# Graph attention, first layer: large piece buffers 7 to 6, small piece buffers 3 to 4, transposed adjacency tiles 3 to 4

## The chip, the cores and the metric

The kernel runs on one core of one Trainium2 chip. Its engines are TensorE (PE in the profile), VectorE (DVE), ScalarE (ACT), GpSimd (POOL) and SyncE (SP, which issues transfers). The metric is the device time of one execution in microseconds; lower is better. Three runs of the kernel before took 3587.35, 3585.51 and 3601.4 us; their median is 3587.35.

## The reference

A graph network of four layers on 3327 nodes with 512 features and a dense 0/1 adjacency matrix. Every layer is `x = x + gnn(relu(layernorm(x)))`. Layers 0 to 2 are graph attention with 8, 4 and 8 heads; layer 3 is a mean over neighbours. The first layer, which the change touches, is

```python
Wh = jnp.einsum('nd,hdo->hno', x, W)             # 8 heads of 64
f1 = jnp.einsum('hno,ho->hn', Wh, a1)
f2 = jnp.einsum('hno,ho->hn', Wh, a2)
e = jax.nn.leaky_relu(f1[:, :, None] + f2[:, None, :], negative_slope=0.2)
e = jnp.where(adj[None, :, :] > 0, e, NEG_INF)
h_prime = jnp.einsum('hnm,hmo->hno', jax.nn.softmax(e, axis=-1), Wh)
out = jax.nn.elu(h_prime)
```

Layer 1 is the same with self loops added to the adjacency and 128 features in each of 4 heads; layer 2 is as layer 0 on other weights; layer 3 multiplies the 0/1 mask with x, divides by the degree and applies three dense matrices.

## The kernel before

**Tiles.** The 3327 nodes make 26 tiles of 128 (the last holds 127). Rows (the attending nodes) are worked off in seven chunks `c`: six of four tiles and one of two. Columns (the attended nodes, tiles `j`) come in five groups `g` of 6, 6, 6, 4 and 4 tiles, the list `JG`; a group of six is called large here, one of four small.

**How softmax becomes matmuls.** The exponential of a leaky relu of a sum is one of two products, depending on the sign of the sum. So `matrices` makes, for a head, a chunk and a group, two 0/2 masks in fp8: `tht` (an edge, and the sum is positive) and `gt` (an edge, and it is not). First `compare` compares the score row `s1b` (a score for each row of the chunk, broadcast over partitions, loaded by `score_rows`, L676) with the column's own score: on ScalarE (L664), for some tiles on VectorE (L661). Then two bitwise operations on VectorE against the adjacency mask `m` split the result: L668 writes `tht`, L670 rewrites `gt`. TensorE multiplies `tht` (L760) and `gt` (L763) with the *pieces*: the features of the column nodes times the two exponentials, each written as three bf16 numbers that add up to the f32 value, so 195 columns for each mask. The pieces of a layer lie in DRAM, a block for each head and group.

**Loops.** For each chunk and each head the five piece blocks are loaded (L714), large groups into tiles with the tag `ab` (600 KB each), small ones into tiles with the tag `abx` (400 KB each). `pieces_tile` chooses the tag: `abx` for a group of four tiles in layer 0, but not for the first head, whose pieces are put together on the chip (`ahead`) and lie in `ab` tiles for all five groups. Then come two passes over the 26 column tiles, one for the first two row tiles of the chunk and one for the other two. Only the very first head of the first chunk is cut in four passes (the last group starts later there). A pass of a full chunk has 104 matmuls, a head 208. A buffer of pieces comes free when the second pass has done its last matmul with it. VectorE then reduces the sums (L778), scales them and divides (L796 to L803) into the chunk's rows `A`.

**What runs beside it.** After each pass `hooks.run` gives out other work: the node stages of the next layer for rows that are done (norm, projection, pieces of the next layer), and in layer 0 the making of the adjacency masks for the next chunk (`mask_steps`): a load of a piece of the adjacency matrix as bf16 (`at`, three buffers, issued by GpSimd, L226), for chunks after the first a transposing DMA into `tr` (issued by SP, L238; the first chunk is transposed by TensorE), a comparison on VectorE (`st`, L245; for a tile on the diagonal also L250 and L251), and a store to DRAM (L252). The masks of a chunk are read back into `m` tiles by SP (L265).

**What sets the order.** The engines run in order. The order on each engine is made when the program is built: a planner takes instructions by their place in the code as soon as their inputs and buffers are free in its own estimate of time. `after(inst, name)` holds an instruction back until another one has been placed; most of the side work is tied in this way to the last matmul of the pass that has just ended (`gone[-1]`). SP's queue carries the loads of pieces, score rows and masks, the transposes, the stores of masks and of the next layer's pieces; an instruction at its head that waits holds up all that follows.

**Memory.** A partition's memory is given out as a stack of pools. `pieces` (the `ab` tiles of layer 0) and `masks` (`at`, `st`, `d`) stand below the pool `first` (the node work before the attention) and, after that is closed, below `att0` (the tiles of layer 0's attention, laid out in the order `A`, `R`, `tht`, `tr`, `abx`, `gt`). After layer 0 all of them are closed, and layer 1's tiles (`att1`) lie on the same addresses; a tile there waits for the tiles below it that were in use.

Of the kernel before, what the change touches and what calls it, by code (L numbers as in the profile page):

```python
# [26 lines left out]
BF16 = mybir.dt.bfloat16  # L27
# [10 lines left out]
P = 128  # L38
# [14 lines left out]
def tile_gnn(ctx: ExitStack, tc: tile.TileContext, x, adj, W0, a01, W1, al, ar, W2, a2,  # L53
# [7 lines left out]
    def pn(t):  # L61
        return min(P, N - t * P)
# [5 lines left out]
    JM = max(n for _, n in JG)  # L68
# [36 lines left out]
    def dims(l):  # L105


        H = heads[l]
        DA = D // H + 1
        AO = -(-(3 * DA + 1) // 8) * 8 if l != 1 else 3 * DA + 1  # L110
        return H, DA, AO, 2 * AO

    abd = []
    for l in range(3):
        H, DA, AO, HW = dims(l)
# [29 lines left out]
    def after(inst, name):  # L145

        tc.add_manual_dep(inst.ins, name, mybir.DependencyInfo(mybir.DependencyClass.NoSync,
                                                               mybir.DependencyReason.SCHED_ONLY))
# [62 lines left out]
    def mask_steps(pool, t, g):  # L211


        n = pn(t)
        c, k = where[t]
        j0, nj = JG[g]
        w = min(nj * P, N - j0 * P)
        q = {}

        def load():  # L220
            at = q["at"] = pool.tile([P, JM * P], BF16, name="at", bufs=3)
            if n < P:
                nc.vector.memset(at, 0.0)
            elif w < nj * P:
                nc.vector.memset(at[:, w:nj * P], 0.0)
            ld = nc.gpsimd.dma_start(at[:n, :w], adj[t * P:t * P + n, j0 * P:j0 * P + w])  # L226
            after(ld, gone[-1] if gone else stored[NT - 1] if c else relus[-3])

        def turn():
            at = q["at"]  # L230
            if c == 0:
                tp = q["tp"] = ps.tile([P, 8, P], BF16, name="tp", bufs=2)
                for j in range(nj):
                    nc.tensor.transpose(tp[:, j, :], at[:, j * P:(j + 1) * P], identb)
                compare()
            else:
                tp = q["tp"] = mp.tile([P, JM, P], BF16, name="tr", bufs=3)
                tr = nc.sync.dma_start(tp[:, :nj], at[:, :nj * P], transpose=True)  # L238
                after(tr, gone[-1] if gone else stored[NT - 1])

        def compare():
            hooks.done += 1
            tp = q["tp"]
            st = masks0[g][:, k] if c == 0 else pool.tile([P, JM, P], FP8, name="st", bufs=3)[:, :nj]
            cm = nc.vector.tensor_scalar(st, tp[:, :nj], 0.0, 2.0, op0=ALU.is_gt, op1=ALU.mult, saturate=False)  # L245
            if gone:
                after(cm, gone[-1])
            if j0 <= t < j0 + nj:
                d = pool.tile([P, P], BF16, name="d", bufs=1)
                nc.vector.tensor_tensor(d, tp[:, t - j0, :], negI, ALU.is_gt)  # L250
                nc.vector.tensor_scalar(dg1[:, t, :], d, 2.0, None, op0=ALU.mult, saturate=False)  # L251
            nc.sync.dma_start(maskd[c][g][:, k], st)  # L252
        return (load, turn) if c == 0 else (load, turn, compare)

    def mask_view(c, g):
# [107 lines left out]
    def pieces(L, t, AB, pool, first, behind=None):  # L363
# [29 lines left out]
        if o == two - 1 and l == 1:  # L393
            for a in range(2):
                L.to_store.append((abd[l][g][:, a, :, js, :].rearrange("h p j w -> p h j w"), pt[:, :, a]))
        elif first and o == two - 1:
            if g not in ahead:
                ahead[g] = pieces_tile(L, bp, g)
            nc.sync.dma_start(ahead[g][:, js], pt[:, 0])
            stored[t] = nc.sync.dma_start(abd[l][g][:, :, js, :].rearrange("h p j w -> p h j w"), pt).ins.name  # L400
        elif o == two - 1:
            L.to_store.append((abd[l][g][:, :, js, :].rearrange("h p j w -> p h j w"), pt))
# [236 lines left out]
    def pieces_tile(L, pool, g):  # L639

        nj = JG[g][1]
        HW = dims(L.l)[3]
        if L.l == 0 and nj == 4 and gone:
            tl = mp.tile([P, nj * HW], BF16, name="abx", bufs=3)
        else:
            tl = pool.tile([P, JM * HW], BF16, name="ab", bufs=7)
        return tl[:, :nj * HW].rearrange("p (j w) -> p j w", j=nj)

    def matrices(L, nt, h, g, s1v, mask, pt, gt):
# [29 lines left out]
    def attention(L, hooks, open_next, close):  # L679
# [5 lines left out]
        for c, (t0, nt) in enumerate(chunks):  # L685
# [3 lines left out]
            for h in range(H):  # L689
# [10 lines left out]
                for a in range(2 if l == 1 else 1):  # L700
                    row = []
                    for g, (_, nj) in enumerate(JG):
                        if l == 1:
                            tl = mp.tile([P, JM * 2 * DA], F32R, name="ab", bufs=7)
                            two = KIND[g] != "b"
                            w = 2 * DA if two else AO
                            v = (tl if two else tl.bitcast(BF16))[:, :nj * w].rearrange("p (j w) -> p j w", j=nj)
                            ld = nc.sync.dma_start(v.bitcast(F32) if two else v, abd[l][g][h, a])
                        else:
                            if g in ahead:  # L710
                                v = ahead.pop(g)
                            else:
                                v = pieces_tile(L, mp if l else bp, g)
                                ld = nc.sync.dma_start(v, abd[l][g][h])  # L714
                        row.append(v)
                    ab.append(row)
# [152 lines left out]
    def lay_out(pool, *tags):  # L869
        for name, n, dt, bufs in tags:  # L870
            pool.tile([P, n], dt, name=name, bufs=bufs)
# [15 lines left out]
    lay_out(rp, ("s1b", WMAX, F32, 2))  # L887
    masking = ExitStack()
    bp = masking.enter_context(tc.tile_pool(name="pieces", bufs=1))
    lay_out(bp, ("ab", JM * 400, BF16, 7))  # L890
    ip = masking.enter_context(tc.tile_pool(name="masks", bufs=1))
    with tc.tile_pool(name="first", bufs=1) as fp:

# [18 lines left out]
        L = open_layer(0)  # L912
# [27 lines left out]
        while hooks.small:  # L940
            hooks.small.pop(0)()
    A, R = [("A", D, F32, n) for n in A_BUFS], ("R", PER * 2 * 129, F32, 1)
    ab, gt, tht = ("ab", JM * 400, BF16, 7), ("gt", PER * JM * P, FP8, 7), ("tht", PER * JM * P, FP8, 7)
    tags = [[A[0], R, tht, ("tr", JM * P, BF16, 3), ("abx", 4 * 400, BF16, 3), gt],
            [A[1], ("ab", JM * 258, F32R, 7), R, ("ts", 2 * JM * P, F32R, 3), ("tv", 2 * 4 * P, F32R, 2), tht[:3] + (10,)],
            [A[2], ab, ("R", PER * 2 * 65, F32, 1), tht, gt]]
    hooks.masks = in_steps([mask_steps(ip, t, g) for t, g in order[20:]])
    for l in range(3):
# [3 lines left out]
        mp = att.enter_context(tc.tile_pool(name=f"att{l}", bufs=1, reuse_waits="tile"))  # L952
# [13 lines left out]
        L = nxt[0]  # L966
# [512 lines left out]
```

## Time and profile before

| what | value |
|---|---|
| median of three runs | 3587.35 us (3585.51 to 3601.4) |
| the profiled execution's own time | 3590.36 us |
| its span | 3588.6 us, mean granted TensorE clock 0.988 |
| TensorE busy | 3452.1 us (96%) |
| weight loads busy | 3112.2 us (87%) |
| VectorE, ScalarE, GpSimd busy | 2622.2, 2507.9, 632.5 us |
| moved by DMA | 797.72 MB, 222 GB/s over the span |
| loads of large pieces in layer 0 and 2 (600 KB, `ab`, SP) | 333, median 5.2 us to landing |
| loads of small pieces in layer 0 (400 KB, `abx`, SP) | 110, median 6.9 us to landing |
| transposing DMAs (`tr`, SP) | 110, median 5.9 us to landing |

How to read it: the profile has a page with the busy time of each engine, the span in 40 slices, the DMA queues, the chain of work that ended last, and the costliest groups of instructions. A group is named by its line, engine, operation and tiles (out<-in). Other views list the instructions of one tile, who waited for whom, the instructions in order of time (start, duration, and in brackets the idle time before one and what ended it), and the busy time of all engines in chosen stretches. Layer 0's attention runs from 163 us to 1249 us of the span, layer 1 from there to about 2090, layer 2 to about 3240, and the last layer's sums to the end. The granted clock is the share of TensorE's full speed that was allowed in a stretch.

### The profile page before, as it was taken

To read this page: it belongs to the slowest core of one execution; us is meant where nothing else is said; L and a number is where in the kernel's file an instruction comes from. 1 tells how busy PE (TensorE), PEld (TensorE's weight loads), DVE (VectorE), ACT (ScalarE), POOL (GpSimd) and SP (SyncE) were. 2 spreads that over 40 slices of the span, in tenths; PEclk is the share of its full clock that TensorE was granted. 3 is DMA by queue.
4 is the path that set the end of the run, shared out by engine and by line. 5 is a ranking of instruction groups with operands and counts; after the bars stand their busy time and mean duration, and the time that the engine had idled before them with its cause. 6 is when DMAs were issued, how large, how long until landed. Compare 5 with 4: busy or idle time off the path is not lost. (4 is left out here: it accounts for less than half of the span.)

```text
span 3588.6 us, 77637 instructions
## 1 busy us (share of the span) xinstructions
PE 3452.1 (96%) x30751; PEld 3112.2 (87%) x30751; DVE 2622.2 (73%) x5227; ACT 2507.9 (70%) x4113; POOL 632.5 (18%) x858
## 2 busy tenths in 40 slices
PE   7889999999999999999999989999999999999998
PEld 6788999999999878888888869989898989876887
DVE  8777878787887789888888868877676767672221
ACT  5767877877887888888798767766676667572111
POOL 6601222111110211233223230001010101020000
PEclk9999999999999999999999999999999999999999
DMA  7798999999966877777877876655555555576331
GB/s 216 235 239 222 237 249 233 258 236 242 262 217 207 283 277 262 282 258 273 283 256 266 307 280 212 195 174 178 176 195 176 173 178 184 166 264 257 122 99 60
DMA packets 398119, 797.72 MB, mean 222 GB/s; under 512 B 112969, under 2 KB 221844, under 8 KB 397104
## 3 DMA queue, kind: packets, MB, share of 16 engines
q1 hardware_dynamic: 363890, 723.14, 62.5%
q0 software_dynamic: 28128, 62.42, 7.5%
q10 hardware_dynamic: 5726, 7.08, 0.6%
q8 instruction: 245, 4.01, 0.5%
q14 instruction: 130, 1.06, 0.1%
HBM read 663.59 MB, written 129.64 MB: 221 GB/s over the span
## 5 line engine op out<-in xcount | busy, mean ns | idle before, releaser
L664 ACT ACTIVATE gt<-s1b,ks 128x512 fp8e4<-128x512 f32 (+1 forms) x2448 | 1448.0, 677 | 294.3 <-issue 160.1
L760 PE MATMUL acc<-ab,tht 128*128 128x195 bf16 (+1 forms) x9112 | 1558.0, 248 | 11.3 <-DVE tht L668 9.2
L763 PE MATMUL acc<-ab,gt 128*128 128x195 bf16 (+1 forms) x9112 | 1557.1, 248 | 5.7 <-DVE rc L800 3.3
L763 PEld LDWEIGHTS <-gt 128*128 128x128 fp8e4 x10744 | 1055.5, 98 | 64.3 <-issue 41.5
L760 PEld LDWEIGHTS <-tht 128*128 128x128 fp8e4 x10744 | 1055.2, 98 | 35.2 <-DVE tht L668 20.0
L668 DVE TENSOR_TENSOR tht<-gt,m 128x768 uint32<-128x768 uint32 (+3 forms) x557 | 449.8, 808 | 121.8 <-ACT gt L664 120.1
L670 DVE TENSOR_TENSOR gt<-tht,m 128x768 uint32<-128x768 uint32 (+3 forms) x557 | 450.1, 808 | 8.7
L633 ACT CAST ts<-tht 128x1536 fp32r<-128x1536 fp8e4 x208 | 300.0, 1470 | 59.0 <-PE acc L753 54.9
L753 PE MATMUL acc<-ab,ts 128*128 128x258 f32 x2496 | 335.0, 290 | 4.9 <-DMA ab<-ab 2.5
L753 PEld LDWEIGHTS acc<-ab,ts 128*128 128x128 f32 x2496 | 314.6, 191 | 14.4 <-issue 3.3
L661 DVE TENSOR_SCALAR gt<-s1b,ns 128x512 fp8e4<-128x512 f32 (+1 forms) x446 | 217.3, 492 | 133.6 <-PE acc L763 127.9
L1015 PE MATMUL acc<-y,mf 128*128 128x512 f32 x1352 | 309.9, 391 | 2.3 <-DVE mf L1010 2.3
L664 ACT ACTIVATE tht<-s1b,ks 128x512 fp8e4<-128x512 f32 (+1 forms) x504 | 308.3, 680 | 2.9 <-DMA s1b<-s 2.4
L763 PE MATMUL acc<-abx,gt 128*128 128x195 bf16 (+1 forms) x1632 | 288.7, 250 | 20.8 <-DVE rc L800 7.8
L760 PE MATMUL acc<-abx,tht 128*128 128x195 bf16 (+1 forms) x1632 | 289.5, 250 | 19.3 <-DMA abx<-ab 15.5
L1015 PEld LDWEIGHTS acc<-y,mf 128*128 128x128 f32 x1352 | 253.6, 188 | 58.5 <-DVE mf L1010 2.7
L863 POOL TENSOR_TENSOR xt<-xt,e 128x512 f32<-128x512 f32 x72 | 122.1, 1695 | 899.6 <-DVE e L862 586.4
L778 DVE TENSOR_REDUCE R<-acc 128x130 f32<-128x390 f32 x416 | 214.7, 556 | 77.5 <-PE acc L763 76.9
L756 PE MATMUL acc<-ab,tht 128*128 128x387 bf16 x1248 | 226.6, 330 | 9.0 <-DMA ab<-ab 5.4
L1012 ACT CAST mf<-m 128x768 fp32r<-128x768 fp8e4 (+1 forms) x78 | 59.1, 762 | 245.8 <-PE acc L1015 234.0
L753 PE MATMUL acc<-ab,tv 128*128 128x258 f32 x1664 | 219.3, 283 | 2.5 <-DVE tv L633 1.4
L753 PEld LDWEIGHTS acc<-ab,tv 128*128 128x128 f32 x1664 | 207.3, 189 | 4.7 <-DVE tv L633 2.5
(163 smaller groups left out, 3722.6 us busy)
## 6 DMA issues: line engine op xcount, KB each, us to landing
ab<-ab SPq DMA_DIRECT2D x333, 600.0 KB, 5.2
ab<-ab SPq DMA_DIRECT2D x112, 774.0 KB, 6.6
ab<-ab SPq DMA_DIRECT2D x112, 516.0 KB, 5.4
ab<-ab SPq DMA_DIRECT2D x112, 400.0 KB, 3.8
abx<-ab SPq DMA_DIRECT2D x110, 400.0 KB, 6.9
ab<-ab SPq DMA_DIRECT2D x56, 582.0 KB, 7.3
s1b<-s SPq DMA_DIRECT2D x120, 256.0 KB, 6.4
m<-mask SPq DMA_DIRECT2D x69, 384.0 KB, 4.1
```

Of the source, the lines that this page charges most:

```text
L633: (nc.scalar.copy if KIND[g] == "s" else nc.vector.tensor_copy)(t[:, :k1 - k0, :nj], th[a][g][:, k0:k1])
L661: nc.vector.tensor_scalar(gv[:, :, jj, :], s1v, L.ns2[:, j, h:h + 1], 2.0, op0=ALU.is_gt, op1=ALU.mult, saturate=False)
L664: nc.scalar.activation(gv[:, :, jj, :], s1v, AF.Relu, bias=L.ks2[:, j, h:h + 1], scale=BIG, saturate=False)
L668: nc.vector.tensor_tensor(pu, gu, mu, ALU.bitwise_and)
L670: nc.vector.tensor_tensor(gu, pu, mu, ALU.bitwise_xor)
L753: mm = nc.tensor.matmul(acc[k][:, :2 * DA], thr[g][:, k - ks[0], jj, :], ab[a][g][:, jj, :], start=(j == 0), stop=(j == NT - 1), skip_grou ...
L756: mm = nc.tensor.matmul(acc[k][:, :3 * DA], th[a][g][:, k, jj, :], ab[a][g][:, jj, :3 * DA], start=(j == 0), stop=(j == NT - 1), skip_grou ...
L760: nc.tensor.matmul(acc[k][:, :3 * DA + o], th[0][g][:, k, jj, :], ab[0][g][:, jj, :3 * DA + o], start=(j == 0), stop=False, skip_group_che ...
L763: mm = nc.tensor.matmul(acc[k][:, AO:AO + 3 * DA + o], th[1][g][:, k, jj, :], ab[0][g][:, jj, AO:AO + 3 * DA + o], start=False, stop=(j == ...
L778: nc.vector.tensor_reduce(R[:, k], v.rearrange("p a (s d) -> p a d s", s=3), AX.X, ALU.add)
L863: nc.gpsimd.tensor_add(xt, xt, e)
L1015: nc.tensor.matmul(acc[k], mf[:, jj, :], y2[g][:, jj, s, :], start=(j0 + jj == 0 and s == 0), stop=(j0 + jj == NT - 1 and s == 1))
```

## The change

In layer 0 the pool `pieces` gets six buffers of 4800 bytes a partition instead of seven, and `pieces_tile` asks for six there; layer 2, which uses the same line, keeps seven. The small pieces `abx` get four buffers of 3200 bytes instead of three, and the transposed adjacency tile `tr` four of 1536 instead of three. No instruction, load or store is added or taken away.

```diff
             else:
-                tp = q["tp"] = mp.tile([P, JM, P], BF16, name="tr", bufs=3)
+                tp = q["tp"] = mp.tile([P, JM, P], BF16, name="tr", bufs=4)
                 tr = nc.sync.dma_start(tp[:, :nj], at[:, :nj * P], transpose=True)
...
         if L.l == 0 and nj == 4 and gone:
-            tl = mp.tile([P, nj * HW], BF16, name="abx", bufs=3)
+            tl = mp.tile([P, nj * HW], BF16, name="abx", bufs=4)
         else:
-            tl = pool.tile([P, JM * HW], BF16, name="ab", bufs=7)
+            tl = pool.tile([P, JM * HW], BF16, name="ab", bufs=6 if L.l == 0 else 7)
...
-    lay_out(bp, ("ab", JM * 400, BF16, 7))
+    lay_out(bp, ("ab", JM * 400, BF16, 6))
...
-    tags = [[A[0], R, tht, ("tr", JM * P, BF16, 3), ("abx", 4 * 400, BF16, 3), gt],
+    tags = [[A[0], R, tht, ("tr", JM * P, BF16, 4), ("abx", 4 * 400, BF16, 4), gt],
```

## The prediction

> **What bounds the kernel now.** I read the page's engine rows and slices first, then the same by stage.
>
> ```profile
> PE 3452.1 (96%) x30751; PEld 3112.2 (87%) x30751; DVE 2622.2 (73%) x5227; ACT 2507.9 (70%) x4113; POOL 632.5 (18%) x858
> ...
> PE   7889999999999999999999989999999999999998
> ...
> DMA  7798999999966877777877876655555555576331
> ```
>
> TensorE is busy 96% of the span, so a change that moves no arithmetic can win only idle time of TensorE: 3588.6 - 3452.1 = 136.5 us in all. The change touches the first layer's attention, 163 to 1249 us. By stretches (after the times: length, TensorE busy, weight loads, VectorE, ScalarE, GpSimd, granted clock, DMA share, GB/s):
>
> ```profile
> 170.00:330.00 160.00, 137.87 (x1508) 132.80 (x1507) 119.38 (x252) 109.92 (x179) 14.52 (x29) 0.94 0.96 239
> 330.00:490.00 160.00, 151.18 (x1659) 147.51 (x1657) 128.09 (x259) 127.84 (x216) 34.40 (x49) 0.99 0.92 237
> 490.00:650.00 160.00, 154.92 (x1702) 151.26 (x1700) 130.30 (x268) 127.60 (x217) 37.29 (x50) 0.98 0.94 238
> 650.00:810.00 160.00, 150.99 (x1666) 147.25 (x1665) 126.46 (x267) 120.24 (x205) 26.25 (x42) 0.99 0.99 248
> 810.00:970.00 160.00, 154.30 (x1719) 151.22 (x1717) 130.35 (x278) 126.46 (x215) 28.67 (x43) 1.00 0.97 253
> 970.00:1130.00 160.00, 160.00 (x1795) 157.71 (x1793) 131.67 (x259) 131.39 (x224) 16.13 (x22) 1.00 0.65 207
> ```
>
> While adjacency is still being transposed (the last one starts at 986.8) TensorE idles 22.1 + 8.8 + 5.1 + 9.0 + 5.7 = 50.7 us and the DMA engines are busy 92 to 99%; when that work ends TensorE does not idle at all. The view of the small piece tile says how much of the 50.7 is a late load:
>
> ```profile
> L714 SPq DMA_DIRECT2D abx<-ab x110: 319/382/1151, 172.1 to 1239.5; - x110
> its engine sat idle before it (us, times) until:
>   DMA abx<-ab: 15.5, 7
>   DVE rc L800: 7.8, 7
>   DVE rc L801: 5.9, 3
> ...
> DMA to landing us min/median/max: 4.7/6.9/11.6
> ```
>
> 15.5 us in seven waits; the list of TensorE's waits has none for a large tile in this layer. One wait, first as SP issues it, then TensorE, then VectorE:
>
> ```profile
> 355.83 0.32 SPq L252 DMA_DIRECT2D mask<-st  x1
> 358.75 1.22 SPq L238 DMA_TRANSPOSE tr<-at  x1
> 360.07 1.26 SPq L714 DMA_DIRECT2D ab<-ab  x2
> 361.43 0.52 SPq L714 DMA_DIRECT2D abx<-ab  x1
> ```
> ```profile
> 368.82 0.24 PE L760 MATMUL acc<-abx,tht 128*128 128x195 bf16 x1 [4.25 <-DMA abx<-ab]
> ```
> ```profile
> 365.45 0.66 DVE L670 TENSOR_TENSOR gt<-tht,m 128x512 uint32<-128x512 uint32 x1
> 366.03 0.16 DVE L800 TENSOR_SCALAR rc<-R 128x4 f32<-128x4 f32 x1
> 369.51 0.29 DVE L250 TENSOR_TENSOR d<-tr,negI 128x128 bf16<-128x128 bf16 x1 [3.32 <-DMA tr<-at]
> ```
>
> SP is in order: it stood at a transpose until 358.7, sent the load at 361.4, TensorE wanted it at 364.6 and had it at 368.8.
>
> **The change: the small pieces.** A head is 208 matmuls in two passes of 104 over the five groups (24, 24, 24, 16, 16), and takes 20.6 us (640 us from 330 to 970 over the 31 heads that finish there). Buffers go round, and one is free when the second pass has left its group. With three small buffers, group 4 of a head takes the one that group 3 of the head before left at matmul 192; it is wanted at matmul 88 of its own head: (208 - 192) + 88 = 104 matmuls, 10.3 us. Group 3 takes that of group 4 two heads back: 208 + 72 = 280 matmuls, 27.7 us. With four, each takes its own group's buffer of two heads back: 16 + 208 + 72 = 296 and 208 + 88 = 296, 29.3 us. A landing took at most 11.6 us and SP's longest single stand at a transpose was 7.6 us; 19.2 us is over 10.3 and under 29.3, so I let all seven waits go.
>
> What is late next is the mask of the same group (L668, L670). For each wait: when TensorE arrived, when L670 of that group ended, and so what is won. Arrived 364.57, ended 366.11, load 368.82: 2.6. Arrived 698.57, ended 699.47, load 701.05: 1.5. Arrived 741.29, ended 741.56, load 742.21: 0.6. Arrived 763.87 and 864.39 with the mask already there: 2.0 and 1.6, all of them. Arrived 256.00 (4.02 lost), but L670 ended only at 263.23, where TensorE stood a second time (3.03): 0. The seventh is 0.2 and goes. Sum: 8.5 us. Upper bound 15.5, if the masks come earlier too; lower bound 0, if the next head's masks give it all back (390.40 shows a mask stall of 1.72 right after the 4.25). ScalarE and VectorE are busy only 80% of these stretches, so they have room to follow: I take 8 of the 8.5.
>
> **The large pieces.** With seven buffers, group 0 takes that of group 2 three heads back: 32 + 416 = 448 matmuls, 44 us; groups 1 and 2: 312 matmuls, 31 us. With six, each takes its own of two heads back: 80 + 208 + 0, 56 + 208 + 24, 32 + 208 + 48: 288 matmuls each, 28.5 us. That is over 19.2 too, so the cost is 0; the cover is those 9 us. If SP stood longer than that, each such head would lose the excess, as the small tile does now (0.2 to 4.3 us). Number and size of loads stay; SP still meets five releases in a head at the same places, only the tile that follows each is another one, so I see nothing that moves the traffic. In the first heads, six loads of large tiles can now go before 186 us instead of seven, and the second head's second piece must wait until the first head leaves its first buffer (171.5, where L714 already waits on TensorE now) and lands by 181 at the 9 us that loads take there; TensorE wants it at about 192. Cost 0; bounds 0 and 10, the latter if it were queued behind the mask store that SP holds until 193.1.
>
> **The fourth transposed tile.** SP waited for a transposed tile's reader only once (1.8 us, L245), so the fourth buffer removes at most that from SP and nothing from TensorE: 0. What VectorE loses on transposes (97.5 us of idle time until one lands) is landing time, which a buffer doesn't shorten. Bounds: if a third of the 31.4 us of TensorE's waits on VectorE in 170 to 970 (9.5 + 8.2 + 7.8 + 5.9) went with it, -10; the loss is the third rival.
>
> **Addresses.** Per partition the large tag gives back 4800 bytes, the others take 3200 + 1536, so the first layer ends 64 bytes lower and its tiles shift by 4800. The second layer's piece tiles lie on them. Now their second load waits until 1263.9 for the last tile's relu (L351), one landing (6.5) before 1270.9, and TensorE loses 1.99 at 1268.72, to a mask. After the shift it is another load of the first four that lies on that tile. Cost 0; bounds -2 (that stall gone) and +8 (one landing exposed, 7.8 being the longest there).
>
> **Sum.** -8 on 3590.36, the profiled execution's own time (span 3588.6 and 1.8 around it): 3582. The median of the runs shown is 3.0 lower, so 3579.
>
> **A page against the rows.** The Trainium skill, page "DMA: Bandwidth & Descriptors", section "Anatomy of one DMA — SWDGE (gpsimd) path", gives 2.0 us plus bytes over 436 GB/s for a transfer. That is fitted on GpSimd's path, and for 0.41 MB the estimate from it would be 2.9 us, which 10.3 us of lead cover several times: by it the change wins nothing and the time is 3587. The trace differs: 6.9 us median, 11.6 at most.
>
> **Rivals.** *The saving is handed on.* The loads come in time, but TensorE then stands at masks whose pace is set by landing transposes. For it: 263.38 and 390.40. Against it: in two of seven cases the mask was long ready. Time 3587. *More than the loads is won.* The whole 15.5 and about a third of the mask waits (10) go, since loads sent a head early leave SP free for transposes: 3587 - 25.5 = 3562. Against it: the same number of issues at the same releases. *Slower: the score row falls behind the transposes.* The order of SP's queue is fixed when the program is planned; with a fourth tile free, transposes may be put ahead of the next head's score row (s1b), each 1.3 us of issue and sometimes a stand for its adjacency. VectorE waited 5.54 us for that row at 254.87, and the mask stall of 3.03 at 263.38 followed. Some 39 heads run beside transposes; a third of them at 3.0 would be +39, less 8: 3618. It decides from 9 heads on (27 - 8 = 19, over 0.5%). Against it: the adjacency tiles that feed transposes stay three, so no more than three can be queued.
>
> **How the numbers follow.** 0.5% of 3587 is 18 us, about what a measurement can tell here. Small waits go, 3579: 0.50. Handed on: 0.20. More: 0.17. Slower: 0.13. Faster by over 18: most of the third case and a little of the first, 0.17. Slower by over 18: most of the fourth, 0.11. Same: 0.72. The range runs from 3562, the third case, to 3601, the handed-on case with an exposed landing (8) and two or three late score rows (6); beyond it lie a few of the third case and most of the fourth.
>
> **What would show it.** Right: TensorE's waits for "abx" go from 15.5 to under 2; the small tile's landing stays near 7; idle time from 170 to 970 falls from 50.7 to about 42; layers 2 to 4 the same within 3 us. Handed on: abx gone, but the waits on L668, L670, L800 and L801 up from 31 to near 40. More: those under 25. Slower: waits of VectorE or ScalarE for s1b, now 13.4 us in four, in many heads. The forecast is wrong if waits for the large tile "ab" appear in the first layer, or if the shift delays the second layer's start past 1270.

## The result, and the profile after

Over twenty runs each, the changed kernel takes 3598.65 us (median; 3585.67 to 3609.55) and the kernel before 3597.72 us (3585.51 to 3611.32). The ratio is 1.0003, with a 95% interval of 0.9992 to 1.0015: no change that can be measured. The three runs of before that the prediction started from had a median 10 us below that of the twenty. The two profiled executions took 3590.36 us (before) and 3600.56 (changed), so the traces are compared by what TensorE waited for, and not by their length.

The page of the changed kernel, busy time and slices:

```profile
PE 3457.0 (96%) x30751; PEld 3114.2 (87%) x30751; DVE 2619.6 (73%) x5227; ACT 2508.1 (70%) x4113; POOL 620.4 (17%) x858
...
PE   7888999999999999999999989999999999999998
...
DMA  7698899999966877777777886655555555576331
```

The same stretches of the first layer (length, TensorE busy, weight loads, VectorE, ScalarE, GpSimd, granted clock, DMA share, GB/s):

```profile
170.00:330.00 160.00, 138.25 (x1524) 133.13 (x1522) 117.50 (x249) 113.27 (x184) 16.20 (x29) 0.96 0.94 240
330.00:490.00 160.00, 148.20 (x1605) 144.62 (x1606) 124.90 (x254) 118.12 (x199) 34.58 (x48) 0.95 0.92 227
490.00:650.00 160.00, 153.00 (x1644) 148.47 (x1642) 126.71 (x262) 125.09 (x214) 35.30 (x50) 0.97 0.96 236
650.00:810.00 160.00, 154.44 (x1711) 150.51 (x1710) 129.30 (x271) 124.94 (x213) 27.49 (x43) 1.00 0.98 252
810.00:970.00 160.00, 154.20 (x1700) 150.87 (x1698) 128.23 (x275) 123.10 (x209) 29.02 (x43) 0.99 1.01 247
970.00:1130.00 160.00, 160.00 (x1795) 157.71 (x1793) 132.86 (x263) 133.15 (x227) 17.01 (x23) 1.00 0.70 218
```

TensorE idles 21.8 + 11.8 + 7.0 + 5.6 + 5.8 = 51.9 us from 170 to 970, where it idled 50.7. The total has not moved, but what it is made of has. The view of the small piece tile, changed kernel:

```profile
L714 SPq DMA_DIRECT2D abx<-ab x110: 319/382/1372, 178.5 to 1239.7; - x110
its engine sat idle before it (us, times) until:
  DVE rc L800: 15.4, 11
  DVE tht L668: 11.3, 11
  DVE gt L670: 5.9, 4
...
DMA to landing us min/median/max: 4.8/7.3/10.5
```

The line that led the list before, 15.5 us until the tile had landed, is gone. The waits on VectorE's masks at the same place have grown instead: L800 from 7.8 to 15.4, L668 to 11.3 (the kernel before had 3.6 there). TensorE's list of waits from 170 to 970 shows the whole of it, before

```profile
PE acc L760 <- DMA abx<-ab: 15.5, 7, 4.3
PE acc L760 <- DVE tht L668: 9.5, 7, 2.8
PE acc L763 <- DVE gt L670: 8.2, 7, 2.4
PE acc L763 <- DVE rc L800: 7.8, 7, 2.1
PE acc L763 <- DVE rc L801: 5.9, 3, 3.0
```

and after:

```profile
PE acc L760 <- DVE tht L668: 17.2, 15, 3.1
PE acc L763 <- DVE rc L800: 15.4, 11, 6.4
PE acc L763 <- DVE gt L670: 8.9, 8, 2.4
PE acc L763 <- DVE rc L801: 4.8, 3, 3.7
```

The four mask waits sum to 31.4 us before and 46.3 after: 15 us more, against 15.5 us of load waits saved. One line more of the list after names a transfer:

```profile
PE acc L760 <- DMA mask<-st: 3.1, 1, 3.1
```

It is a mask wait as well. The matmul began at 328.75, 0.06 us after L668 had ended and before the named mask store landed, and VectorE had stood 5.13 us at L245 (until 327.32) ahead of that L668. With it the mask waits are 49.4 us.

The places agree too. Numbering the 208 matmuls of a head from 0, all 15.5 us of the load's waits before lie at matmul 88, the first of the second small group, and the waits put down to VectorE or ScalarE at matmuls 88 and 89 (the first of each mask in that group) are 24.3 us. In the changed kernel the load has none, and the other waits at these two places are 41.5 us.

The longest, 6.40 us, tells how one comes about. VectorE in the changed kernel, in order of time, and then TensorE:

```profile
391.17 0.69 DVE L796 TENSOR_TENSOR R<-R,cpm 128x520 f32<-128x520 f32 x1
396.89 0.43 DVE L245 TENSOR_SCALAR st<-tr 128x512 fp8e4<-128x512 bf16 x1 [5.02 <-DMA tr<-at]
397.23 0.42 DVE L798 TENSOR_TENSOR R<-R 128x260 f32<-128x260 f32 x1
397.57 0.69 DVE L670 TENSOR_TENSOR gt<-tht,m 128x512 uint32<-128x512 uint32 x1
398.17 0.16 DVE L800 TENSOR_SCALAR rc<-R 128x4 f32<-128x4 f32 x1
```
```profile
398.40 0.32 PE L763 MATMUL acc<-abx,gt 128*128 128x195 bf16 x1 [6.40 <-DVE rc L800]
```

VectorE works its queue in order. It stood 5.02 us at the comparison of a transposed adjacency tile that had not landed; behind it in its queue was L670, which finishes the mask that TensorE needs next. (The profile names L800, the instruction right after.) VectorE's own list, changed kernel, from 170 to 970:

```profile
DVE st L245 <- DMA tr<-at: 74.9, 25, 7.7
DVE d L250 <- DMA tr<-at: 37.8, 13, 6.6
```

That is 112.7 us of standing at transposes; before it was 62.9 + 33.4 = 96.3. (Standing here means that VectorE is idle at the head of its queue until a transfer has landed.) So the question for the runs: does this standing eat what the small buffers save?

### The profile page after: what moved, and what is told of

It reads as the page before. It is cut to its first block, busy times and chain, and to the rows that moved or that the text cites. A ratio compares the mean times of both kernels' runs of the same rounds, so it can differ in the third digit from the quotient of the medians.

```text
span 3598.7 us, 77661 instructions
## 1 busy us (share of the span) xinstructions
PE 3457.0 (96%) x30751; PEld 3114.2 (87%) x30751; DVE 2619.6 (73%) x5227; ACT 2508.1 (70%) x4113; POOL 620.4 (17%) x858
## 5 line engine op out<-in xcount | busy, mean ns | idle before, releaser
L668 DVE TENSOR_TENSOR tht<-gt,m 128x768 uint32<-128x768 uint32 (+3 forms) x557 | 446.5, 802 | 118.4 <-ACT gt L664 116.8
L670 DVE TENSOR_TENSOR gt<-tht,m 128x768 uint32<-128x768 uint32 (+3 forms) x557 | 449.5, 807 | 8.7
L763 PE MATMUL acc<-abx,gt 128*128 128x195 bf16 (+1 forms) x1632 | 289.4, 250 | 27.1 <-DVE rc L800 15.4
L760 PE MATMUL acc<-abx,tht 128*128 128x195 bf16 (+1 forms) x1632 | 290.2, 250 | 14.4 <-DVE tht L668 11.3
```

What stands on the lines that cost most here:

```text
L668: nc.vector.tensor_tensor(pu, gu, mu, ALU.bitwise_and)
L670: nc.vector.tensor_tensor(gu, pu, mu, ALU.bitwise_xor)
L760: nc.tensor.matmul(acc[k][:, :3 * DA + o], th[0][g][:, k, jj, :], ab[0][g][:, jj, :3 * DA + o], start=(j == 0), stop=False, skip_group_che ...
L763: mm = nc.tensor.matmul(acc[k][:, AO:AO + 3 * DA + o], th[1][g][:, k, jj, :], ab[0][g][:, jj, AO:AO + 3 * DA + o], start=False, stop=(j == ...
```

## The experiments

Theory: two streams were late for TensorE at the same place, the start of the second small group: the piece and the mask. A fourth small buffer mends the first; the second, held up by VectorE's standing, takes its place. Rivals: the seven mask buffers and ScalarE pace the masks; the DMA engines set the pace of everything; the small buffers are worth nothing in any case. All times below are against runs of the kernel before on the same chip.

### The standing taken away, with four and with three small buffers

These two leave out that the masks of the second to the last chunk come from the adjacency: VectorE compares a tile of ones. All transfers stay. The edit, on the changed kernel and on the kernel before:

```diff
-    nc.vector.memset(ones_row, 1.0)
+    nc.vector.memset(ones_row, 1.0); ones_tr = const.tile([P, P], BF16, name="ones_tr"); nc.vector.memset(ones_tr, 1.0)
...
-            tp = q["tp"]
+            tp = q["tp"] if c == 0 else ones_tr[:, None, :].to_broadcast([P, JM, P])
```

> The changed kernel, with one thing left out: for the chunks after the first, VectorE compares a tile of ones in place of the transposed adjacency, so it never stands until a transpose has landed (the masks are then all full; every transfer and every instruction stays). Theory (the load waits were replaced by mask waits, because VectorE stands in order at late transposes, 114 us in the changed kernel): both kinds go. TensorE's idle time from 170 to 970 us falls from 52 us to under 20, waits for the small piece stay at 0, and the time is 30 to 45 us under the kernel before. Rival (the masks are paced by ScalarE and by the seven mask buffers): idle time stays over 35 us and the time within 10 us of before. Rival (the DMA engines, 92 to 101% busy there, set the pace): waits for pieces come back, 20 us or more, and the gain stays under 15 us.

Measured: 3531.05 us against 3591.53, ratio 0.9830 (0.9812 to 0.9847). The stretch from 170 to 970:

```profile
170.00:970.00 800.00, 791.84 (x8920) 779.39 (x8919) 683.29 (x1380) 659.15 (x1113) 152.33 (x223) 1.00 1.02 263
```

TensorE idles 8.2 us in place of 51.9, and got through 8920 matmuls in that time in place of 8175. The gain, 60 us, is more than the 30 to 45 expected. Part of it is not idle time: for the same 30751 matmuls TensorE is busy 3434.5 us of the whole execution, 3457.0 in the changed kernel and 3452.1 before, and its granted clock from 170 to 970 us is 1.00, 0.97 and 0.98. Why the clock is higher where TensorE stands less no run here tells.

> The kernel before, with the same left out: VectorE compares a tile of ones in place of the transposed adjacency. Theory: the mask waits go (31 us to under 12), the waits for the small piece stay or grow (15.5 us to 15 to 30, since TensorE now comes earlier), and the time is 15 to 30 us under the kernel before: 8 to 15 us over the same with four small buffers. Rival (mask buffers and ScalarE): within 10 us of before. Rival (the small buffers are worth nothing even then): the same time as with four small buffers, within 4 us.

Measured: 3554.31 us, ratio 0.9884 (0.9867 to 0.9901). TensorE's waits in the same stretch:

```profile
PE acc L760 <- DMA abx<-ab: 15.2, 6, 4.9
PE acc L763 <- DVE gt L670: 2.4, 2, 1.8
```

The gain, 37 us, is over the 15 to 30 expected. The masks come in time and the small piece's waits are there again. Four small buffers are now worth 23 us (8 to 15 expected), where they were worth nothing with the standing. TensorE's idle time differs by 12.9 us of these, its busy time by 9.6 (3444.1 and 3434.5). Neither the mask buffers nor ScalarE pace the bulk of this, since neither was touched. And the DMA engines, at a share of 1.02 with 263 GB/s against 0.96 with 241 in the changed kernel, had room for the faster pace.

### The standing avoided: a later comparison

Nothing is left out from here on. An empty step between transpose and comparison:

```diff
-        return (load, turn) if c == 0 else (load, turn, compare)
+        return (load, turn) if c == 0 else (load, turn, lambda: None, compare)
```

> The kernel before, with one empty step between a transpose and its comparison, so that VectorE comes to a transposed tile about a quarter of a head later; nothing is left out. Theory: VectorE's standing at transposes falls from 97 us to under 30, TensorE's mask waits fall with it, the small piece's waits of 15 us stay; 10 to 25 us under the kernel before. Rival (mask buffers and ScalarE pace the masks): standing falls but TensorE's idle time doesn't; within 6 us of before.

> The changed kernel with the same empty step; nothing is left out. Theory: neither the load waits nor most of the mask waits are left; TensorE's idle time from 170 to 970 us falls from 52 to 15 to 25 us, and the time is 20 to 40 us under the kernel before, 8 to 15 us under the same step with three small buffers. Rival (mask buffers and ScalarE): within 6 us of before. Rival (the small buffers are worth nothing): equal to the step with three small buffers within 4 us.

Measured: 3558.62 us with three small buffers, ratio 0.9910 (0.9894 to 0.9926); 3554.12 us with four, 0.9888 (0.9871 to 0.9904). The first gain, 33 us, is over the 10 to 25 that I expected, the second, 37 us, lies in the 20 to 40; the 4.5 us between them is under the 8 to 15 expected, and it is not told apart from nothing by these intervals. VectorE's list with four small buffers shows what is left:

```profile
DVE d L250 <- DMA tr<-at: 52.5, 15, 7.3
...
DVE st L245 <- DMA tr<-at: 3.7, 1, 3.7
```

The standing at L245 has all but gone. That at L250, the diagonal's comparison in the same step, is still there, 52.5 us where the changed kernel had 37.8 (with three small buffers 35.4, and 33.4 before): it is not tied to a pass as L245 is, so the planner puts it where it believes the tile to have landed, and the empty step doesn't reach it. TensorE idles 24.1 us with four buffers, none of it for the small piece; with three 23.6, of which 11.7 for the small piece.

### The diagonal tied as well

On top of the empty step:

```diff
-                nc.vector.tensor_tensor(d, tp[:, t - j0, :], negI, ALU.is_gt)
+                dd = nc.vector.tensor_tensor(d, tp[:, t - j0, :], negI, ALU.is_gt); gone and after(dd, cm.ins.name)
```

> The changed kernel with the empty step, and the diagonal's comparison (L250) held back until the comparison beside it (L245); nothing is left out. In the run with the step alone VectorE stood no more than 3.7 us at L245 but 52.5 us at L250, which the planner places as soon as it believes the transpose landed. Theory: that was the rest of the mask waits. Standing at transposes falls under 10 us, TensorE's waits on VectorE from 170 to 970 us fall from 21 to under 9, and the time is 10 to 20 us under the step alone, 48 to 58 us under the kernel before, near the run with a tile of ones (60 under). Rival (mask buffers and ScalarE set what is left): standing falls but the time is within 5 us of the step alone.

> The kernel before with the empty step and the tied diagonal, three small and seven large buffers; nothing is left out. Theory: the mask waits go and the waits for the small piece stay, 12 to 16 us in six or so; 35 to 42 us under the kernel before, and 10 to 22 us slower than the same with four small and six large buffers. Rival (the small buffers are worth nothing): the same time as with four, within 4 us.

Measured: 3545.39 us with four, ratio 0.9873 (0.9852 to 0.9894), and 3550.60 with three, 0.9883 (0.9862 to 0.9904), against 3590.27. The standing at L250 is gone and L245 has 4.7 us, but I had not counted L223 and L225, the zeroing of the adjacency tile's padding, which stands on VectorE until a transpose has read that tile: 20.1 us with four. The pair differs by 5.2 us, still under the theory's 10 to 22, and the intervals overlap. Against the empty step alone the tie adds about 5 us with four (0.9873 and 0.9888), not the 10 to 20 expected, and here too the intervals overlap; TensorE's waits on VectorE fell to 18 us, not under 9. So this step by itself does not tell the theory from its rival.

### The padding off VectorE

On top of both, for the chunks after the first:

```diff
-                nc.vector.memset(at, 0.0)
+                (nc.gpsimd if c else nc.vector).memset(at, 0.0)
...
-                nc.vector.memset(at[:, w:nj * P], 0.0)
+                (nc.gpsimd if c else nc.vector).memset(at[:, w:nj * P], 0.0)
```

> The changed kernel with the empty step, the tied diagonal, and the zeroing of the adjacency tile's padding (L223, L225) on GpSimd instead of VectorE for the chunks after the first; nothing is left out. With the first two VectorE still stood 20 us there until a transpose had read the tile. Theory: that goes too, TensorE's waits on VectorE from 170 to 970 us fall from 17 to about 10, and the time is 3 to 10 us under the run without this step, 48 to 55 us under the kernel before. Rival (GpSimd now holds the adjacency loads back, since it stands where VectorE stood): within 3 us of the run without it, or slower.

> The same three steps on the kernel before, three small and seven large buffers. The two pairs with real masks gave 4.5 and 5.2 us between three and four small buffers, the pair with a tile of ones 23. Theory: as VectorE gets freer the pair moves towards the 23; 8 to 15 us slower than with four. Rival (with real masks the fourth buffer is worth about 5 us at most): 2 to 6 us slower.

Measured: 3538.78 us with four, ratio 0.9834 (0.9817 to 0.9851), and 3556.06 with three, 0.9886 (0.9871 to 0.9901), against 3595.09. With four that is 56 us under the kernel before, where 48 to 55 was expected. Now the pair is 17 us apart (8 to 15 expected) and the intervals don't touch. TensorE's waits with three

```profile
PE acc L760 <- DMA abx<-ab: 13.4, 6, 7.2
PE acc L760 <- DVE tht L668: 4.4, 3, 2.2
```

and the longest ones with four:

```profile
PE acc L763 <- DVE gt L670: 5.3, 3, 2.4
PE acc L760 <- DVE tht L668: 4.1, 4, 1.6
```

With four the load's waits are not replaced by anything. GpSimd stands 106 us at L223 and L225 instead of VectorE, and the kernel is faster all the same, so the first rival falls as well. The second, that the fourth buffer is worth 2 to 6 us with real masks, falls.

### The tie alone

The tied diagonal on the changed kernel, without the empty step (edit as above).

> The changed kernel with the diagonal's comparison held back until the one beside it, without the empty step. Theory: VectorE stands at L245 instead, which it reaches right after the same pass; of the 113 us of standing from 170 to 970 us at most the 38 at L250 go, and the time is 0 to 12 us under the changed kernel. If the diagonal alone were the cause, it would come near the run with both, 45 us under.

Measured: 3591.22 against 3595.09, ratio 0.9993 (0.9982 to 1.0003). L250 no longer stands, L245 does for 76.2 us, and TensorE idles 46.5 us. The diagonal alone was not the cause.

### More mask buffers

On the kernel before, eight of each mask in the first layer; the room comes from a large piece buffer:

```diff
-bufs=10 if l == 1 else 7)
+bufs=10 if l == 1 else 8 if l == 0 else 7)
...
-name="gt", bufs=7)
+name="gt", bufs=8 if l == 0 else 7)
...
-name="ab", bufs=7)
+name="ab", bufs=6 if L.l == 0 else 7)
...
```

> The kernel before with eight buffers each for the two masks in the first layer instead of seven, three small pieces, three transposed tiles, six large pieces; nothing is left out. Rival theory (seven mask buffers pace the masks): mask waits fall from 31 us to under 15, 10 to 25 us under the kernel before. My theory (standing at transposes sets them): the standing stays near 97 us, the mask waits fall by a third at most, and the time is within 10 us of the kernel before.

Measured: 3602.24 against 3590.27, ratio 1.0026 (1.0011 to 1.0041). Its small piece tile:

```profile
its engine sat idle before it (us, times) until:
  DMA abx<-ab: 43.1, 17
  DVE tht L668: 8.4, 2
```

The rival was right on the masks and wrong on the time. From 170 to 970 the waits on VectorE fell from 35 us to 15, although VectorE still stood 102 us at transposes, so deeper mask buffers cover that standing in part; the waits for the small piece rose from 15.5 to 42.5. It is the mirror image of the change: mend the mask alone and the load takes its place. Why it takes more than it gave is open: this kernel also has one large buffer fewer, and its order of instructions differs on every engine but little on TensorE. The trace shows that SP came later to the pieces: it waited for TensorE to leave a buffer 54 times (59.6 us) from 170 to 970, before 85 times (94.3 us). Eight mask buffers together with four small ones, with VectorE left standing, were not run.

### One part of the change alone

Four small and six large buffers, but three transposed tiles:

```diff
-tp = q["tp"] = mp.tile([P, JM, P], BF16, name="tr", bufs=4)
+tp = q["tp"] = mp.tile([P, JM, P], BF16, name="tr", bufs=3)
...
```

> One part alone: four small and six large buffers, three transposed tiles. The instructions stand in the same order on every engine as in the changed kernel with four. Both theories: the same time as the changed kernel, so within 5 us of the kernel before; the waits for the small piece are gone and the mask waits are 45 to 55 us from 170 to 970 us. If the fourth transposed tile did cost something, this one is over 5 us faster.

Measured: 3596.94 against 3590.27, ratio 1.0015 (1.0002 to 1.0029); no wait for the small piece, 51.1 us of idle time, 46.2 on the four mask lines. The 6.7 us over the kernel before are a little more than the 5 expected. The changed kernel had 1.0003 (0.9992 to 1.0015) and 51.9: the intervals overlap. In the two traces the instructions start in the same order on every engine, but for one pair of neighbours on VectorE (L225 and L250) that start within 0.06 us of each other.

### The freed kernel with an eighth mask buffer

The freed kernel with four small buffers, the fourth transposed tile given up for an eighth `gt`:

```diff
-name="tr", bufs=4)
+name="tr", bufs=3)
...
-name="gt", bufs=7)
+name="gt", bufs=8 if l == 0 else 7)
...
```

> The freed kernel (empty step, tied diagonal, padding on GpSimd, four small and six large buffers) with the fourth transposed tile given up and an eighth buffer for the second mask (gt) in the first layer instead; nothing is left out. TensorE still waited 12 us for masks there from 170 to 970 us. If the mask buffers set that rest, it falls under 6 us and the time is 3 to 8 us under the freed kernel, 60 to 65 us under the kernel before. If it is VectorE's order of work, nothing changes: within 3 us of the freed kernel, 53 to 60 us under the kernel before; that the fourth transposed tile is given up costs nothing in either case.

Measured: 3530.77 against 3596.39, ratio 0.9819 (0.9806 to 0.9833), the fastest of all with real masks. TensorE idles 10.3 us in place of 12.3. The interval overlaps that of the freed kernel, so what the eighth buffer adds is not settled; the waits on the masks fell from 10.8 us to 6.5, not under the 6 expected if the mask buffers set that rest.

### All together

Idle time of TensorE from 170 to 970 us, what of it waited for pieces, and VectorE's standing at L245 and L250 there, each from one profiled execution:

| kernel | small buffers | ratio to before | idle | for pieces | standing |
|---|---|---|---|---|---|
| before | 3 | 1 | 50.7 | 15.5 | 96.3 |
| changed | 4 | 1.0003 | 51.9 | 0 | 112.7 |
| later comparison | 3 | 0.9910 | 23.6 | 11.7 | 38.3 |
| later comparison | 4 | 0.9888 | 24.1 | 0 | 56.2 |
| and tied diagonal | 3 | 0.9883 | 26.9 | 15.6 | 2.2 |
| and tied diagonal | 4 | 0.9873 | 18.3 | 0 | 4.7 |
| and padding on GpSimd | 3 | 0.9886 | 25.5 | 13.4 | 3.9 |
| and padding on GpSimd | 4 | 0.9834 | 12.3 | 0 | 2.8 |
| tile of ones | 3 | 0.9884 | 21.1 | 15.2 | none |
| tile of ones | 4 | 0.9830 | 8.2 | 0 | none |

In the last rows of both kinds the idle time of three exceeds that of four by 13 us, nearly the load's waits; in the first pair, and with the later comparison alone, by nothing.

## Why the prediction was wrong, point by point

**The forecast, 3579.** It was a small gain of 8 us; measured was no change, which is the first rival, the saving handed on. The two medians of twenty differ by 0.9 us. That 3598.65 lies in the range of 3562 to 3601 is luck: 10 us of the distance to 3579 are the three runs that it started from, and the upper end was added up from causes that did not occur (an exposed landing, late score rows).

**All seven waits for the small piece go.** Right, and by the count of matmuls between two uses of a buffer: 15.5 us to none, with a landing of 7.3 us median in place of 6.9.

**The sum of 8.5 us over the single waits, and "they have room to follow: I take 8 of the 8.5".** This is the step that failed. I compared each load with the mask of the same group and took all else as fixed. VectorE and ScalarE were called free because they are busy 80% of the time. But VectorE's idle time was not room: of 165 us from 170 to 970 in the kernel before, 96 were spent at the head of an in-order queue, waiting for transposes to land, with the masks behind. The 97.5 us stood in the prediction, as landing time that a buffer does not shorten; I did not ask what was queued behind it. When TensorE came to the masks earlier it found them no earlier: VectorE stood 112.7 us at the same transposes in place of 96.3. The runs with a tile of ones and with the freed VectorE show it: without the standing, the same buffers are worth 23 and 17 us, and nothing takes the place of the load's waits.

**"Can win only idle time of TensorE: 136.5 us in all."** Too narrow. In the freed kernel with an eighth `gt` TensorE's busy time is 3432.8 us, 19.3 under the kernel before, for the same 30751 matmuls, with a granted clock of 1.00 in place of 0.98 from 170 to 970 us. It did not decide this forecast, since the changed kernel idles as long as the kernel before.

**Large pieces, cost 0.** Right: no wait for a large tile in the first layer, in the changed kernel and with 60 us less time for the same loads. **The fourth transposed tile, 0.** Right, as far as the run without it tells: it was not faster. **The shift of addresses, 0.** Right, and as foreseen it is another load: the second layer's second load now goes at 1271.23, after the relu (L351) of the last tile but one (ended 1271.20), and the third at 1276.71, after that of the last tile (1275.80); before, the second waited for the last tile's and went at 1264.02. TensorE's stall at the second layer's first masks is 2.00 us, 1.99 before, and that layer's first matmul comes 4.72 us after the last relu in both. It starts at 1280.52, past the 1270 that the prediction named as a sign against it, but because the first layer's attention ended later in this profiled execution (it began 4.5 us later and took 7.3 us longer), not by the shift. From there to the end it is 2318 us, 2320 before.

**The rivals.** "Handed on" had a chance of 0.20 and came about, with the marks given for it: waits on L668, L670, L800 and L801 from 31 to 46 (49 with the wait put down to the mask store). Its "against", that in two of seven cases the mask was long ready, was a look at single cases, too. "More than the loads" needed transposes to move, and their standing grew instead. "Slower" did not show: VectorE's waits for the score row are not in the list of the changed kernel.

**The page.** The estimate of 2.9 us for a landing, worked out from the Trainium skill's page "DMA: Bandwidth & Descriptors", section "Anatomy of one DMA — SWDGE (gpsimd) path", would have given no change. No change came, but not for that reason: before, the load was late and stopped TensorE for 15.5 us, and a load of 400 KB took 6.9 us (median) to land, 7.3 in the changed kernel.

## What to carry to other kernels

When two things arrive late at the same instruction, mending one can show nothing; test it together with the other, as in the pairs here (0 and 17 us for the same buffers). Where an engine works its queue in order, as VectorE does here, its idle share is room only if it waits for nothing with work queued behind: look at what it stands at and what is next in its queue. Side work that waits for a transfer belongs late in that queue, all of its instructions, the small ones for padding and the diagonal too.

## What was not expected

The empty step took the standing from L245, which is tied to a pass, and left it at its untied neighbour L250: 37.8 us there without the step, 52.5 with it (four small buffers; 33.4 and 35.4 with three). The best kernel tried is 1.8% faster than the kernel before (0.9819), all of it from the order on VectorE, the zeroing moved to GpSimd, and buffers; the DMA engines, which I read as nearly full at 0.92 to 0.99, carried 261 GB/s in place of 241 from 170 to 970.
